# Three edits to a bidirectional recurrent stack with a ternary FFN: the fold's sums on VectorE, small statistics on GpSimd, and an earlier end of the last FC chunks

## The chip, the cores and the metric

The kernel runs on one core of a Trainium2 chip. Its time is device microseconds of one execution, and the median of a few executions is quoted. Of the kernel before there are three timed runs (1719.25, 1719.33 and 1719.43 us) and one execution under the hardware profiler. The core has a matrix engine (TensorE, PE in the profile), a vector engine (VectorE, DVE), an activation engine (ScalarE, ACT), a general engine (GpSimd, POOL) and a queue engine that issues transfers (SyncE, SP). Each engine takes its instructions in order and waits for the others by semaphores.

## The reference

The input x has 8 sequences of 512 tokens with 512 features. Two residual blocks are applied in turn. Norms without gamma and beta are plain.

```
h0   = layernorm(x)
fwd  = stack(h0);  bwd = flip(stack(flip(h0)))        # the same weights in both directions
stack: for i in 0..3:
    z  = sigmoid(h @ Wz[i].T + bz[i]);  t = tanh(h @ Wh[i].T + bh[i])
    a  = clip(1 - z);   h_new = linear_scan(a, z * t)     # along the tokens
    h  = layernorm(h_new + (h if i > 0 else 0)) * gamma + beta
x    = x + concat(fwd, bwd) @ fusion_W + fusion_b
g    = gelu(layernorm(x) @ ternary(W_fc).T);  x = x + (layernorm(g) * ln_w + ln_b) @ ternary(W_proj).T
```

Wz and Wh are one and the same matrix here, and so are bz and bh. A layer thus has one product u, and its three gate factors a, t and z all come from that u. ternary() rounds a matrix to -1, 0, 1 by a threshold from its mean absolute value.

## The kernel before

**Tiles.** 512 features make four chunks (NC_ = 4) of 128 partitions, 512 tokens make four tiles (NT = 4), and the 2048 hidden features of the FFN make 16 chunks (NF). The state of one sequence in one direction, called an item here, is kept with features on partitions (h, 128x4x512), as the scan along the tokens wants it. The layernorm needs tokens on partitions, so each layer ends with a turn there and back.

**Slots.** The recurrent stage is written out by hand as a list of slots (`slot`, L439). A slot of a layer issues one chunk of the product (`gates`, L456: four fp32 matmuls, each of which PE runs as two passes of 512 columns), the three activations of that chunk (`factors`, L475), VectorE's clamp and product (`product`, L483), the scan (L489) and the residual addition (L548). Beside that it takes shares of the norm of an item before it (`shares`, L258). Eight sequences run in four pairs. In a pair, each layer runs over four items: both directions of both sequences.

**The norm.** `norm` (L340) queues four token tiles and then four feature chunks. For each tile, PE makes four transposes into PSUM (pt, L316; two buffers). `stats` (L168) has VectorE find mean and variance (bn_stats, bn_aggr into mv, L171 and L173), add the epsilon (ve, L177) and negate the mean (nmu, L182), and GpSimd take the power -0.5 (rs, L178). `normalise` (L185) then has ScalarE multiply nmu by rs (nmr, L188) and write the normalised tile to SBUF (tok, L189). When four such tiles exist, PE turns them back (pf, L325) and ScalarE applies gamma and beta (L331). In most slots one tile is turned. In some, called two-tile slots here, two tiles are turned; PE's queue then holds transposes behind the second of them which wait for a tok. The same `stats` serves the tokens of x at the front (rx), the last layer, where only rs is wanted (rsv, since the norm's shift is folded into the fusion's weights), and the tokens of y in the FFN (rs_y, nmr_y; `y_stats` and `y_tokens`, L923 to L931).

**The fold.** The last layer's gamma, beta and mean are folded into the fusion's weights fw (two directions of four chunks of 128x512) and bias fb. `fold_sums` (L663) makes PE sum each direction's fw, weighted by gamma and by beta, over all 512 rows: four fp32 matmuls into pfold, copied to SBUF by ScalarE (L673). It is called after layer 1 of the first two items. The tile `both` (L119, filled at L729) holds the weights; the two `fpick` tiles choose a row. `fold` (L675), in layer 2, spreads the mean over the partitions with one matmul (pm, L678) and has VectorE correct the four chunks (L682). `fold_bias` (L685) does the same for the bias with two matmuls (pb, L688) and an addition (L689). The two sums sit in tok buffers meanwhile, and the counter `held` says so to the slots, which admit a new token tile only below 10.

**The rest of the recurrent stage.** `fusion` (L567) multiplies the last layer's states by fw (pu, L582), and VectorE scales by rsv and adds (L592). The first layer of the next pair (L504) is interleaved with it. Work on the FFN's weights (absolute sums, thresholds, ternary values) is taken in pieces along the recurrent stage.

**The FFN.** One step per hidden chunk: `fc` (L831) makes eight passes on PE (ph, L836), ScalarE's gelu, square and scaled copy (ghi), and VectorE's two running sums (L851) and glo (L853). Two steps later `proj` (L858) makes eight passes into the four po tiles. `token_stats` (L868) turns the running sums into a mean and a scale for each token. At the end of the list the FC chunks are doubled up in two steps (L939), so that `token_stats` of the last sequence comes two steps before the end (L943). `center` (L893) and `finish_last` (L915) are VectorE's last work on each token tile, and `store` (L900) sends the tile out on SP's queue.

Of the kernel before, what the change touches and what calls it, by code (L numbers as in the profile page):

```python
# [9 lines left out]
F32 = mybir.dt.float32  # L10
F32R = mybir.dt.float32r
AF = mybir.ActivationFunctionType
ALU = mybir.AluOpType
# [3 lines left out]
P = 128  # L17
# [7 lines left out]
def kernel(  # L25
# [84 lines left out]
    fb = const.tile([P, H], F32, name="fb")  # L110
    lnw = const.tile([P, NF], F32, name="lnw")
    lnb = const.tile([P, NF], F32, name="lnb")

# [2 lines left out]
    nc.vector.memset(warm, 0.0)  # L116
    ones = const.tile([P, P], F32, name="ones")
    nc.vector.memset(ones, 1.0)
    both = const.tile([P, NC_, 2, 64], F32, name="both")  # L119
    picks = []  # L120
    for i in range(2):
        s = const.tile([P, P], F32, name=f"fpick{i}")
        nc.vector.memset(s, 0.0)
        nc.vector.memset(s[64 * i : 64 * i + 1, :], 1.0 / H if i else 1.0)
        picks.append(s)


    xT[0] = hp.tile([P, NC_, S], F32, tag="h", name="xT_0")
# [39 lines left out]
    def stats(src, name, rs=None, shift=True):  # L168

        st = small.tile([P, 6], F32, tag="st", name=f"st_{name}")  # L170
        nc.vector.bn_stats(st, src)  # L171
        mv = small.tile([P, 2], F32, tag="mv", name=f"mv_{name}")
        nc.vector.bn_aggr(mv, st)  # L173
# [3 lines left out]
        nc.vector.tensor_scalar(ve, mv[:, 1:2], LN_EPS, None, ALU.add)  # L177
        nc.gpsimd.tensor_tensor(rs, ve, mhalf, ALU.pow)  # L178
        if not shift:
            return rs, None  # L180
        nmu = small.tile([P, 1], F32, tag="nmu", name=f"nmu_{name}")
        nc.vector.tensor_scalar(nmu, mv[:, 0:1], -1.0, None, ALU.mult)  # L182
        return rs, nmu

    def normalise(dst, src, rs_nmu, name):  # L185
        rs, nmu = rs_nmu
        nmr = small.tile([P, 1], F32, tag="nmr", name=f"nmr_{name}")
        nc.scalar.activation(nmr, nmu, AF.Copy, scale=rs)  # L188
        nc.scalar.activation(dst, src, AF.Identity, bias=nmr, scale=rs)  # L189

    def ternary(dst, w, hi_lo):
# [37 lines left out]
    with rec:  # L229
# [428 lines left out]
                extra.append([None, lambda hi=hi, lo=lo, v=v: nc.vector.tensor_tensor(lo, v, hi.bitcast(F32), ALU.subtract)])  # L658


        folded = {}

        def fold_sums(d):  # L663

            ps = ps_u.tile([P, H], F32, tag="u", name=f"pfold_{d}")
            for c in range(NC_):
                nc.tensor.matmul(
                    ps, lhsT=both[:, c, :, :].rearrange("p i r -> p (i r)"), rhs=fw[:, d * NC_ + c, :],
                    start=(c == 0), stop=(c == NC_ - 1),
                )  # L670
            folded[d] = tokp.tile([P, H], F32, tag="tok", name=f"fold_{d}")
            held[0] += 1
            nc.scalar.copy(folded[d], ps)  # L673

        def fold(d):  # L675

            pm = ps_u.tile([P, H], F32, tag="u", name=f"pm_{d}")
            nc.tensor.matmul(pm, lhsT=picks[1], rhs=folded[d], start=True, stop=True)  # L678
            for c in range(NC_):
                def chunk(c=c):  # L680
                    w = fw[:, d * NC_ + c, :]
                    nc.vector.scalar_tensor_tensor(w, w, gam[:, c : c + 1], pm, ALU.mult, ALU.subtract)  # L682
                stages.append((now[0] + c, "resid", chunk))

        def fold_bias():  # L685
            pb = ps_u.tile([P, H], F32, tag="u", name="pb")
            for d in range(2):
                nc.tensor.matmul(pb, lhsT=picks[0], rhs=folded[d], start=(d == 0), stop=(d == 1))  # L688
            nc.vector.tensor_tensor(fb, pb, fb, ALU.add)  # L689
            held[0] -= 2  # L690


        def load_pair(use, b):
# [34 lines left out]
        for i, v in enumerate((bet, gam)):  # L728
            nc.vector.tensor_copy(both[:, :, i, :], v.unsqueeze(2).broadcast_to([P, NC_, 64]))  # L729
        for b in range(0, B, 2):  # L730
            last_pair = b + 2 == B
            if b == 0:
                for name, part in (("fc", fc_part), ("pw", proj_part)):
                    for i in range(NW):
                        absolute(part, i, name)
                    tots = []
                    extra.append([None, lambda n=name, tots=tots: tots.append(total(n))])
                    extra.append([None, lambda n=name, tots=tots: threshold(n, tots[0])])
                for name, part in (("fc", fc_part), ("pw", proj_part)):
                    for i in range(NW):  # L740
                        quantised(part, i, name)
            for l in range(1, L):
                if last_pair:
                    load_fc(l - 1)
                    if l == 1:
                        combined()
                        load_pw(0)
                for s in ((b, 0), (b, 1), (b + 1, 0), (b + 1, 1)):
                    if l == L - 1 and not last_pair and s[1] == 0:
                        norm_x(s[0] + 2, now[0])  # L750
                    if l == L - 1 and s[1] == 0:
                        load_pair("f", s[0])
                    if l == L - 2 and not last_pair and s[1] == 1:
# [7 lines left out]
                    if b == 0 and l == 1 and s[0] == 0:  # L761
                        fold_sums(s[1])
                    if b == 0 and l == 2:
                        if s[0] == 0:
                            fold(s[1])
                        elif s[1] == 0:
                            fold_bias()
            if last_pair:
                load_fc(L - 1)


            firsts = [] if last_pair else first_layer(b + 2) + first_layer(b + 3)
            for i in range(2):
                for t, tile_ in enumerate(fusion(b + i)):
                    slot(tile_, 2, True)
                    for _ in range(2 if i == 0 and t % 2 == 0 else 1):
                        if firsts:
                            slot(firsts.pop(0))
                if last_pair and i == 0:
                    load_pw(1)  # L780
                    load_pw(2)
# [132 lines left out]

    def finish_last(b, t):  # L915
        row = xs["y", b, t]
        nc.vector.scalar_tensor_tensor(row, po[b][t], stat[b][0][:, t : t + 1], row, ALU.mult, ALU.add)
        store(b, t)

    rests = []  # L920
    found, ytok = {}, {}
# [97 lines left out]
```

## Time and profile before

| | us |
|---|---|
| median of three runs | 1719.33 |
| the profiled execution's own time | 1719.44 |
| its span in the profile | 1717.4 |
| time of that execution outside the span | 2.0 |
| PE busy | 1705.8 |
| VectorE busy | 1449.8 |
| ScalarE busy | 1072.3 |
| GpSimd busy | 214.5 |

| stretch, us | PE busy | VectorE busy | ScalarE busy | GpSimd busy |
|---|---|---|---|---|
| 0 to 62 (loads, first layer) | 57.62 | 50.11 | 40.92 | 10.63 |
| 62 to 111 (pair 0, layer 1) | 47.56 | 42.97 | 39.55 | 8.43 |
| 111 to 230 (pair 0, layers 2 and 3) | 118.86 | 109.84 | 102.27 | 19.41 |
| 230 to 1222 (pairs 1 to 3 and fusions) | 990.8 | 876.8 | 597.3 | 148.4 |
| 1222 to 1717 (FFN) | 491.00 | 370.02 | 292.32 | 27.63 |

In a line of the groups, the form is: source line, engine, operation, output and input by the program's names, sizes, count, then the busy time in us and the mean in ns of one instruction, then the idle time of the engine just before such instructions and what ended it. In a timeline, each line has start and duration in us. A line with a count above one stands for several instructions that followed each other without a gap.

### The profile page before, as it was taken

What the parts mean: (1) busy time and instruction counts of PE and PEld (TensorE: products, weight loads), DVE (VectorE), ACT (ScalarE), POOL (GpSimd) and SP (SyncE); (2) the same over time, 40 slices, a digit from 0 to 9 for tenths busy, and PEclk for the clock granted to TensorE, in tenths of its full rate; (3) what the DMA queues carried; (4) which work ended last, traced back from release to release, by engine and by line L of the source; (5) the groups of instructions that cost most, each with busy time, mean ns of one, the idle gap of its engine ahead of it and who ended that gap; (6) DMA issues with size and microseconds to landing.
All of it is one profiled execution on the core that took longest, in us unless ns stands there. A gap on an engine that the chain in (4) does not pass through costs nothing.

```text
span 1717.4 us, 19766 instructions
## 1 busy us (share of the span) xinstructions
PE 1705.8 (99%) x6442; PEld 1042.8 (61%) x6442; DVE 1449.8 (84%) x2859; ACT 1072.3 (62%) x1851; POOL 214.5 (12%) x334
## 2 busy tenths in 40 slices
PE   9999999999999999999999999999999999999998
PEld 4455554555555455555545555554688888888887
DVE  7989989889998998999899899996568768768876
ACT  5898883468886246888624688861266566566654
POOL 2111111111111111111111111110000000000000
PEclk9999999999999999999999999999999999999999
DMA  7002221160000115000012200202201101100100
GB/s 270 19 25 81 99 86 43 56 202 1 1 13 19 56 59 199 1 1 19 13 55 68 105 15 35 74 1 98 74 1 49 50 1 50 50 19 32 50 19 31
DMA packets 46455, 91.75 MB, mean 53 GB/s; under 512 B 5264, under 2 KB 5264, under 8 KB 45328
## 3 DMA queue, kind: packets, MB, share of 16 engines
q1 hardware_dynamic: 45632, 89.18, 15.3%
q10 hardware_dynamic: 720, 1.31, 0.2%
q8 instruction: 51, 0.84, 0.2%
q14 instruction: 52, 0.43, 0.1%
HBM read 65.30 MB, written 25.17 MB: 53 GB/s over the span
## 4 chain that ended last, share of the span: by engine, by line
PE 85%; DVE 9%; issue 4%; ACT 1%; DMA 1%; POOL 0%; DVEq 0%; POOLq 0%; ACTq 0%; SPq 0%
PE u L461 33%; PE pu L582 12%; PE ph L836 12%; PE po L863 12%; PE pt L316 6%; PE u L504 5%; PE pf L325 4%; DVE z L489 2%; DVE st L171 1%; DVE z L485 1%; PE py L214 1%; DVE zf L489 1%; DVE z L548 1%; DVE a L484 1%; DMA xT<-in_xt_dram 0%
## 5 line engine op out<-in xcount | busy, mean ns | idle before, releaser
L461 PE MATMUL u<-h,gw 128*128 128x512 f32 x768 | 345.5, 592 | 0.0
L461 PE MATMUL u<-xT,gw 128*128 128x512 f32 x768 | 345.4, 593 | 0.0
L489 DVE TENSOR_TENSOR_SCAN z<-a,z 128x512 f32<-128x512 f32 x224 | 274.1, 1224 | 7.6
L840 ACT ACTIVATE g<-ph 128x512 f32<-128x512 f32 x128 | 76.4, 597 | 240.6 <-PE ph L836 240.6
L461 PEld LDWEIGHTS u<-h,gw 128*128 128x128 f32 x768 | 138.7, 190 | 139.2 <-issue 138.9
L461 PEld LDWEIGHTS u<-xT,gw 128*128 128x128 f32 x768 | 138.7, 190 | 139.2 <-issue 138.2
L478 ACT ACTIVATE a<-u,ngb 128x512 f32<-128x512 f32 x192 | 131.6, 685 | 142.2 <-PE u L461 141.6
L171 DVE BATCH_NORM_STATS2 st<-pt 128x6 f32<-128x512 f32 x256 | 177.1, 692 | 40.5 <-PE pt L316 40.1
L178 POOL TENSOR_TENSOR rs<-ve,mhalf 128x1 f32<-128x1 f32 x192 | 123.2, 642 | 702.8 <-DVE nmu L182 669.9
L863 PE MATMUL po<-pwq,ghi 128*128 128x512 f32 x512 | 203.5, 398 | 0.0
L836 PE MATMUL ph<-yhi,fcq 128*128 128x512 f32 x512 | 199.7, 390 | 0.0
L863 PE MATMUL po<-pwq,glo 128*128 128x512 f32 x512 | 199.6, 390 | 0.0
L836 PE MATMUL ph<-ylo,fcq 128*128 128x512 f32 x512 | 199.4, 389 | 0.0
L485 DVE TENSOR_TENSOR z<-z,t 128x512 f32<-128x512 f32 x224 | 153.4, 685 | 9.1 <-ACT z L480 9.1
L189 ACT ACTIVATE tok<-pt,nmr,rs 128x512 f32<-128x512 f32 x192 | 149.2, 777 | 6.4
L851 DVE TENSOR_TENSOR acc<-acc,g 128x512 f32<-128x512 f32 x112 | 77.3, 690 | 87.9 <-ACT g L840 87.0
L480 ACT ACTIVATE z<-u,gb 128x512 f32<-128x512 f32 x192 | 132.2, 689 | 0.0
L479 ACT ACTIVATE t<-u,gb 128x512 f32<-128x512 f32 x192 | 130.7, 681 | 0.0
L316 PEld LDWEIGHTS pt<-ident,z 128*128 128x128 f32 x640 | 78.6, 141 | 79.7 <-issue 47.7
L504 PE MATMUL u<-xT,gw 128*128 128x512 f32 x256 | 114.8, 593 | 0.8 <-DVE gw L711 0.8
L582 PE MATMUL pu<-fw,xT 128*128 128x512 f32 x256 | 115.2, 593 | 0.0
L582 PE MATMUL pu<-fw,h 128*128 128x512 f32 x256 | 115.1, 592 | 0.0
(147 smaller groups left out, 2558.5 us busy)
## 6 DMA issues: line engine op xcount, KB each, us to landing
xn<-in_x_dram SPq DMA_DIRECT2D x32, 256.0 KB, 4.4
xf<-in_x_dram SPq DMA_DIRECT2D x32, 256.0 KB, 5.5
x<-xf SPq DMA_DIRECT2D x32, 256.0 KB, 2.0
xy<-x SPq DMA_DIRECT2D x32, 256.0 KB, 4.4
out_dram<-xy SPq DMA_DIRECT2D x32, 256.0 KB, 2.0
xT<-in_xt_dram SPq DMA_DIRECT2D x7, 1024.0 KB, 7.5
fca<-in_fc_wT_dram SPq DMA_DIRECT2D x16, 256.0 KB, 3.0
pwa<-in_proj_wT_dram SPq DMA_DIRECT2D x16, 256.0 KB, 2.6
```

The source lines that it names most:

```text
L171: nc.vector.bn_stats(st, src)
L189: nc.scalar.activation(dst, src, AF.Identity, bias=nmr, scale=rs)
L316: nc.tensor.transpose(pt[:, ts(c, P)], zs[c][:, ts(t, P)], ident)
L461: nc.tensor.matmul(u, lhsT=gw[l][:, c, ts(o, P)], rhs=h[:, c, :], start=(c == 0), stop=(c == NC_ - 1),)
L478: nc.scalar.activation(a, u, AF.Sigmoid, bias=ngb[:, l, o : o + 1], scale=-1.0)
L480: nc.scalar.activation(z, u, AF.Sigmoid, bias=gb[:, l, o : o + 1])
L485: nc.vector.tensor_tensor(z, z, t, ALU.mult)
L489: nc.vector.tensor_tensor_scan(dst[:, d], a[:, d], z[:, d], 0.0, ALU.mult, ALU.add)
L504: nc.tensor.matmul(u, lhsT=gw[0][:, c, ts(o, P)], rhs=xT[b][:, c, :], start=(c == 0), stop=(c == NC_ - 1),)
L582: nc.tensor.matmul(pu, lhsT=hs[d][:, c, ts(t, P)], rhs=fw[:, d * NC_ + c, :], start=(c == 0), stop=(c == NC_ - 1),)
L836: nc.tensor.matmul(ph, lhsT=w, rhs=ys[b][c][i], start=(c == 0 and i == 0), stop=(c == NC_ - 1 and i == 1),)
L863: nc.tensor.matmul(po[b][t], lhsT=part[:, ts(t, P)], rhs=pwq[k // NP_][:, k % NP_, :], start=(k == 0 and i == 0), stop=(k == NF - 1 and i ...
```

## The change

It has three parts, in one diff.

**The fold.** `fold_sums`, `fold` and `fold_bias` are replaced by one function `fold()`, which is called once, after layer 1 of the first item. It queues 16 VectorE instructions of 128x512, one for every second slot: for each direction, four that sum gamma times chunk into `sum_g`, and four that sum beta times chunk into `sum_b`. These are sums over chunks alone; the sum over partitions is left to the matmul that spreads it. After each direction's sums `centred` issues the one pm matmul and queues the four corrections of fw; last comes `bias` with one pb matmul. The tile `both`, its two copies and the fpick tiles go; `mean_of` and `sum_b` come.

**The statistics.** In `stats`, ve is made by GpSimd, nmu is gone, and nmr is made by GpSimd as mean times rs times -1. `normalise` is left with one ScalarE instruction.

**The end.** The doubling of FC chunks starts two steps earlier and covers three steps; `token_stats` of the last sequence comes one step earlier. The last token tile is finished in two halves, the second half stored from ScalarE's queue. The pool of ghi and glo has six buffers instead of five.

```diff
-    both = const.tile([P, NC_, 2, 64], F32, name="both")
-    picks = []
...
+    mean_of = fusp.tile([P, P], F32, name="mean_of")
+    nc.vector.memset(mean_of, 1.0 / H)
+    sum_b = fusp.tile([P, H], F32, name="sum_b")
...
-        nc.vector.tensor_scalar(ve, mv[:, 1:2], LN_EPS, None, ALU.add)
+        nc.gpsimd.tensor_scalar(ve, mv[:, 1:2], LN_EPS, None, ALU.add)
         nc.gpsimd.tensor_tensor(rs, ve, mhalf, ALU.pow)
         if not shift:
             return rs, None
-        nmu = small.tile([P, 1], F32, tag="nmu", name=f"nmu_{name}")
-        nc.vector.tensor_scalar(nmu, mv[:, 0:1], -1.0, None, ALU.mult)
-        return rs, nmu
...
-        nc.scalar.activation(nmr, nmu, AF.Copy, scale=rs)
+        nc.gpsimd.tensor_scalar(nmr, mv[:, 0:1], rs, -1.0, ALU.mult, ALU.mult)
+        return rs, nmr
...
-        folded = {}
-        def fold_sums(d):
...
+        def fold():
+            sum_g = qp.tile([P, H], F32, tag="q", name="sum_g")
+            at = [now[0]]
+            def later(f):
+                stages.append((at[0], "resid", f))
+                at[0] += 2
+            def summed(dst, w, v, first):
+                if first:
+                    later(lambda: nc.vector.tensor_scalar(dst, w, v, None, ALU.mult))
+                else:
+                    later(lambda: nc.vector.scalar_tensor_tensor(dst, w, v, dst, ALU.mult, ALU.add))
+            def centred(d):
+                pm = ps_u.tile([P, H], F32, tag="u", name=f"pm_{d}")
+                nc.tensor.matmul(pm, lhsT=mean_of, rhs=sum_g, start=True, stop=True)
+                for c in range(NC_):
...
+                    stages.append((now[0] + c, "resid", chunk))
+            def bias():
+                pb = ps_u.tile([P, H], F32, tag="u", name="pb")
+                nc.tensor.matmul(pb, lhsT=ones, rhs=sum_b, start=True, stop=True)
+                nc.vector.tensor_tensor(fb, pb, fb, ALU.add)
             for d in range(2):
+                for dst, v in ((sum_g, gam), (sum_b, bet)):
+                    for c in range(NC_):
+                        summed(dst, fw[:, d * NC_ + c, :], v[:, c : c + 1], c == 0 and (dst is sum_g or d == 0))
+                later(lambda d=d: centred(d))
+                at[0] += NC_ - 2
+            later(bias)
...
-    partp = ctx.enter_context(tc.tile_pool(name="parts", bufs=5, reuse_waits="tile"))
+    partp = ctx.enter_context(tc.tile_pool(name="parts", bufs=6, reuse_waits="tile"))
...
-        nc.vector.scalar_tensor_tensor(row, po[b][t], stat[b][0][:, t : t + 1], row, ALU.mult, ALU.add)
-        store(b, t)
+        for h in range(2 if t == NT - 1 else 1):
+            cols = slice(h * H // 2, (h + 1) * H // 2) if t == NT - 1 else slice(0, H)
+            nc.vector.scalar_tensor_tensor(
+                row[:, cols], po[b][t][:, cols], stat[b][0][:, t : t + 1], row[:, cols], ALU.mult, ALU.add
+            )
+            (nc.scalar if h else nc.sync).dma_start(out=out[b, ts(t, P), cols], in_=row[:, cols])
...
-        for _ in range(2 if ends - 4 <= j < ends - 2 else 1):
+        for _ in range(2 if ends - 6 <= j < ends - 3 else 1):
...
-        if j == ends - 2:
+        if j == ends - 3:
             late.append(token_stats(b))
```

More of the change, by code (lines that the diff above doesn't have):

```diff
@@ L109 @@
     bet = const.tile([P, NC_], F32, name="bet")
-    fb = const.tile([P, H], F32, name="fb")
+    fb = fusp.tile([P, H], F32, name="fb")
     lnw = const.tile([P, NF], F32, name="lnw")
@@ L118 @@
     nc.vector.memset(ones, 1.0)
-    both = const.tile([P, NC_, 2, 64], F32, name="both")
-    picks = []
[L121 to L125, printed above, removed]
+    mean_of = fusp.tile([P, P], F32, name="mean_of")
+    nc.vector.memset(mean_of, 1.0 / H)
+    sum_b = fusp.tile([P, H], F32, name="sum_b")
     xT[0] = hp.tile([P, NC_, S], F32, tag="h", name="xT_0")
@@ L180, in stats, with normalise @@
             return rs, None
-        nmu = small.tile([P, 1], F32, tag="nmu", name=f"nmu_{name}")
-        nc.vector.tensor_scalar(nmu, mv[:, 0:1], -1.0, None, ALU.mult)
-        return rs, nmu
-    def normalise(dst, src, rs_nmu, name):
-        rs, nmu = rs_nmu
         nmr = small.tile([P, 1], F32, tag="nmr", name=f"nmr_{name}")
-        nc.scalar.activation(nmr, nmu, AF.Copy, scale=rs)
+        nc.gpsimd.tensor_scalar(nmr, mv[:, 0:1], rs, -1.0, ALU.mult, ALU.mult)
+        return rs, nmr
+    def normalise(dst, src, rs_nmr, name):
+        rs, nmr = rs_nmr
         nc.scalar.activation(dst, src, AF.Identity, bias=nmr, scale=rs)
@@ L658, in combined @@
                 extra.append([None, lambda hi=hi, lo=lo, v=v: nc.vector.tensor_tensor(lo, v, hi.bitcast(F32), ALU.subtract)])
-        folded = {}
-        def fold_sums(d):
[L665 to L686, printed above, removed]
-            for d in range(2):
-                nc.tensor.matmul(pb, lhsT=picks[0], rhs=folded[d], start=(d == 0), stop=(d == 1))
-            nc.vector.tensor_tensor(fb, pb, fb, ALU.add)
-            held[0] -= 2
+        def fold():
[13 more added lines that the diff above has]
+                for c in range(NC_):
+                    def chunk(c=c):
+                        w = fw[:, d * NC_ + c, :]
+                        nc.vector.scalar_tensor_tensor(w, w, gam[:, c : c + 1], pm, ALU.mult, ALU.subtract)
+                    stages.append((now[0] + c, "resid", chunk))
[3 more added lines that the diff above has]
+                nc.vector.tensor_tensor(fb, pb, fb, ALU.add)
+            for d in range(2):
+                for dst, v in ((sum_g, gam), (sum_b, bet)):
[4 more added lines that the diff above has]
+            later(bias)
@@ L727 @@
             slot(work, 4 if i == NC_ + 1 else 2, i > NC_ + 1)
-        for i, v in enumerate((bet, gam)):
-            nc.vector.tensor_copy(both[:, :, i, :], v.unsqueeze(2).broadcast_to([P, NC_, 64]))
         for b in range(0, B, 2):
@@ L760 @@
                     layer(s, l)
[L761 to L767, printed above, removed]
+                    if (b, l, s) == (0, 1, (0, 0)):
+                        fold()
             if last_pair:
```

## The prediction

> **What bounds the kernel now.** I read the busy shares and the chain of waits first, then PE's own waits, then the groups that the diff touches, and last the timeline where PE waits.
>
> ```profile
> PE 1705.8 (99%) x6442; PEld 1042.8 (61%) x6442; DVE 1449.8 (84%) x2859; ACT 1072.3 (62%) x1851; POOL 214.5 (12%) x334
> ...
> PE 85%; DVE 9%; issue 4%; ACT 1%; DMA 1%; POOL 0%; DVEq 0%; POOLq 0%; ACTq 0%; SPq 0%
> ```
>
> PE is busy for 1705.8 of 1717.4 us. So a pass removed from PE is worth its time, unless PE then waits, and any new wait of PE is a loss. PE's waits, by what ended them (total us, times, longest):
>
> ```profile
> PE pt L316 <- ACT tok L189: 2.5, 7, 0.6
> PE pt L316 <- DVE z L489: 1.3, 1, 1.3
> ...
> PE pf L325 <- ACT tok L189: 0.4, 1, 0.4
> ```
>
> The commonest wait is that of transposes for tok, the end of the chain of statistics that the diff rebuilds. The groups that it touches:
>
> ```profile
> L178 POOL TENSOR_TENSOR rs<-ve,mhalf 128x1 f32<-128x1 f32 x192 | 123.2, 642 | 702.8 <-DVE nmu L182 669.9 <-DVE a L484 15.9 <-ACT z L480 12.1
> L188 ACT ACTIVATE nmr<-nmu,rs 128x1 f32<-128x1 f32 x192 | 56.7, 295 | 74.6 <-POOL rs L178 64.9 <-DVE st L171 5.7 <-DVE xf L592 1.6
> L177 DVE TENSOR_SCALAR ve<-mv 128x1 f32<-128x1 f32 x256 | 39.3, 153 | 26.3 <-DVE mv L173 0.5
> L182 DVE TENSOR_SCALAR nmu<-mv 128x1 f32<-128x1 f32 x192 | 27.6, 144 | 0.5 <-issue 0.5
> L667 PE MATMUL pfold<-fw,both 128*128 128x512 f32 x16 | 7.2, 592 | 0.0
> L682 DVE SCALAR_TENSOR_TENSOR fw<-fw,gam,pm 128x512 f32<-128x512 f32 x8 | 5.9, 740 | 0.0
> L688 PE MATMUL pb<-fold,fpick 128*128 128x512 f32 x4 | 1.9, 593 | 0.0
> ```
>
> A two-tile slot, in the timeline from 371.5 us on. The second tile's mean and variance are there at 372.43 (bn_aggr from 372.25, 0.18 long):
>
> ```profile
> 371.69 0.55 POOL L178 TENSOR_TENSOR rs<-ve,mhalf 128x1 f32<-128x1 f32 x1 [3.40 <-DVE nmu L182]
> ...
> 372.67 0.42 DVE L484 TENSOR_SCALAR a<-a 128x512 f32<-128x512 f32 x1
> 372.84 0.66 POOL L178 TENSOR_TENSOR rs<-ve,mhalf 128x1 f32<-128x1 f32 x1 [0.60 <-DVE nmu L182]
> ...
> 373.00 0.69 DVE L485 TENSOR_TENSOR z<-z,t 128x512 f32<-128x512 f32 x1
> ...
> 373.72 1.23 DVE L489 TENSOR_TENSOR_SCAN z<-a,z 128x512 f32<-128x512 f32 x1
> 373.85 0.78 ACT L189 ACTIVATE tok<-pt,nmr,rs 128x512 f32<-128x512 f32 x1
> ...
> 374.69 0.66 PE L316 MATMUL pt<-ident,z 128*128 128x128 f32 x4 [0.23 <-ACT tok L189]
> ```
>
> The second power takes 0.66 us, not 0.55. It began inside the clamp `a`, and it ended at 373.50, which is 0.41 after the clamp's end at 373.09. Begun inside a scan, a power takes longer still (timeline at 38 us), though GpSimd has the same work:
>
> ```profile
> 38.24 1.45 POOL L178 TENSOR_TENSOR rs<-ve,mhalf 128x1 f32<-128x1 f32 x1 [0.59 <-DVE nmu L182]
> ```
>
> So GpSimd is stopped by the VectorE instruction in flight. That is the one thing in the profile that speaks against this change.
>
> **What the Trainium skill says.** "SBUF — State Buffer", section "Who interferes with whom": a VectorE instruction with two SBUF inputs, or one in a two-port mode, holds a port which GpSimd's reads need, and the other "fully blocks". The trace agrees: 0.55 us beside bn_stats, which reads PSUM, 0.66 and 1.45 us beside the clamp and the scan, and the clamp keeps its 0.42. "GPSIMD Engine Reference", section 2.1 "Instruction dispatch": the next GpSimd instruction does not wait for the one before, so a dependent one needs a semaphore wait; the built order of the changed kernel has these waits between ve, power and nmr. "Perfetto Trace Analysis", section "GPSIMD Engine Instruction": GpSimd's spans are unreliable, so I use them against VectorE's ends only.
>
> **The fold.** PE loses two pfold groups of eight passes and two of pb's four: 18 passes. A pass counts start to start, not by its 592 ns: pfold runs from 88.58 us and the next product starts at 92.02, so 3.44 us for eight, 0.43 each, and 18 x 0.43 = 7.74 us. ScalarE loses two copies of 0.58, VectorE two of 0.28. VectorE gains 16 instructions of 128x512. No such sum is in the trace; the nearest row, L682, takes 740 ns, and bounds from the clamp (0.42) to L194's like form (0.75) would give 6.7 to 12 us. I take 16 x 0.74 = 11.8 us. One falls in every second slot, so 0.37 us a slot. A slot lasts 4.31 us on PE (eight passes, 3.44, and eight transposes of 0.109), and VectorE is busy 110 of 119 us in 111 to 230: about 0.33 us a slot free. That isn't enough alone, but the second part gives back more, so I cost the sums at nothing. Without that cover they would cost 16 x 0.74 - 40 slots x 0.33, about nothing to 2 us. The corrections and pm move later, still ahead of the fusion; they keep their price. With the sums out of the tok pool, one transpose tile comes a slot sooner: nothing.
>
> **The statistics.** VectorE loses ve (0.15) on every tile and nmu (0.14) on most. Start to start, bn_aggr to ve takes 0.29 us (372.25 to 372.54) and nmu to the next 0.06, so 0.33 to 0.42 us leave a tile's chain, about 0.35 a slot with one tile: as much as the fold's sums take. ScalarE loses 224 nmr of 0.295, 66 us, which lie beside PE's work and are no gain as such. GpSimd gets 317 ve and 224 nmr. A 128x1 tensor_scalar on GpSimd isn't in the trace: from below, its memset of the same size takes 98 ns; from above, the power 0.55. I take 0.1 to 0.2, nearer to the memset; the skill's only GpSimd timings are for long rows, and don't help.
>
> What matters is when tok can start. Behind nmr, ScalarE's in-order queue holds tok and then the next slot's a, t and z, for which VectorE waits; behind a late ve, GpSimd's queue holds the next tile's three instructions. In a one-tile slot the turn back waits for a tok made a slot earlier, about 1.0 us of room: most of a delay is hidden, and I leave 0.3 us for the few slots without room. In a two-tile slot the second tok is on PE's path. With GpSimd never stopped: bn_aggr's end 372.43, 0.15 for the semaphore, ve 0.1, power 0.55, nmr 0.1 and two handovers of 0.03: tok at 373.4 instead of 373.85. PE had waited 0.23, so the slot gains up to 0.3. With GpSimd stopped at each step: ve in the clamp, the power in the product, nmr in the scan, so tok 0.41 after the scan's end. VectorE is 0.35 earlier by then: (373.72 + 1.23 - 0.35) + 0.41 = 375.0, which is 1.2 us later than before. So a two-tile slot costs -0.3 to +1.2, and I take +0.3: ve may get through in the gap ahead of the clamp, and then the power ends where it did. I count 12 such slots with PE near its wait: nine in the first pair (at about 41, 47, 73, 78, 84, 89, 103, 108 and 125 us), and one in each later first layer (at about 374, 672 and 971). That is 12 x 0.3 = 3.6 us.
>
> **The end.** Last, in the timeline:
>
> ```profile
> 1711.57 2.72 DVE L917 SCALAR_TENSOR_TENSOR xy<-po,rsg,xy 128x512 f32<-128x512 f32 x4
> ...
> 1712.34 2.31 SPq L901 DMA_DIRECT2D out_dram<-xy  x4
> ```
>
> The last pass starts at 1712.61, ends at 1713.0, and VectorE finishes at 1714.29. It is late because `center` ran to 1711.65. A step of eight passes is 8 x 0.227 = 1.82 us, so statistics one step sooner let each finish start at its tile's end, and the last half ends about 0.9 us after PE instead of 1.3. The half-size store is shorter too. ScalarE's queue is empty there, so its store waits behind nothing. Bounds 0.4 to 1.0; I take 0.7. The passes that move are the same in number, and the sixth buffer keeps the third early chunk from waiting.
>
> **Sum,** against the profiled execution's 1719.44: -7.74 + 3.6 + 0.3 - 0.7 = -4.5, so 1714.9 us; against the median of 1719.33, 1714.8.
>
> **Rivals.** (A) GpSimd is hardly stopped: two-tile slots at -0.1 on average, nothing in the others: -7.74 - 1.2 - 0.7 = -9.6, so 1709.8. For it: the short instructions may slip between two of VectorE's. Against it: 0.66 and 1.45. (B) GpSimd is stopped three times in each two-tile slot: 12 x 1.2 = 14.4, with 1.1 in the one-tile slots ahead of norms without room: -7.74 + 15.5 - 0.7 = +7.1, so 1726.5. It is slower from 0.7 us a slot on, and by more than 0.2% from 1.0 on. For it: VectorE's clamp, product, scan and addition follow without a gap. Against it: PE's waits there were below 0.6, and a slot late by 1.2 leaves the next with fewer things to wait for. (C) The fold's gain isn't realised: at 63.9 us, VectorE runs without a gap from 65 to 71, so PE that comes 3.44 sooner only waits for z: -4.5 + 3.4, so 1718.3, no change that can be told.
>
> **How the numbers follow.** A measurement of this kernel can tell about 0.2%, 3.4 us, from no change: below 1715.9 is faster, above 1722.8 slower. Chances: my forecast 0.35 (its own range 1711 to 1719), A 0.25, B 0.25, C 0.15. Of the forecast's 0.35, 0.24 lie below 1715.9; A gives 0.25; C 0.02: faster 0.51. C's rest and the forecast's rest give 0.22 for no change with 0.02 of B; slower is the rest, 0.27 with C's tail. A with the end at 1.0 and its slots at -0.2 gives 1708.3, and B with every slot stopped gives 1726.5, beyond which other stages would have to be late too. The range from 1708.5 to 1726.5 leaves out about half of B and a little of A, 0.15 to 0.2.
>
> **What would show it.** PE busy must fall by about 7.7 (the fold). PE's waits for tok should total 4 to 7 us instead of 2.9; near 15 is B, below 2 is A. In a two-tile slot, the time from bn_aggr's end to the second tok was 1.42 us: 1.0 is A, near 1.7 mine, 2.6 B. The waits of PE for z in the first 111 us tell C. The time from PE's last pass to the end of the span, 4.4 us, should become 3.7. I am wrong if GpSimd's tensor_scalar takes over 0.4, or if VectorE becomes late in 77 to 230 us.

## The result, and the profile after

The changed kernel takes 1743.83 us (median of 4 runs, 1743.39 to 1745.07) against 1719.37 us of the kernel before in the same sessions (1719.25 to 1719.43). The ratio is 1.0143, with a 95% interval of 1.0126 to 1.0161. It is 24.5 us slower. The forecast was 1714.8, with a range that ended at 1726.5.

The page of the changed kernel, busy shares and chain:

```profile
PE 1708.1 (98%) x6424; PEld 1042.3 (60%) x6424; DVE 1403.3 (81%) x2330; ACT 1007.7 (58%) x1625; POOL 474.5 (27%) x875
...
PE 56%; issue 22%; POOL 14%; DVE 4%; ACT 3%; DMA 1%; POOLq 0%; DVEq 0%
```

VectorE and ScalarE have less to do, as the diff intends (46.5 and 64.6 us less). GpSimd has 260 us more. GpSimd had 0% of the chain that ended last before; now it has 14%. PE has 18 passes fewer, and yet is busy 2.3 us longer: some passes ran at half the clock (below). PE's waits, total, times and longest:

```profile
PE pt L310 <- ACT tok L183: 15.7, 14, 4.0
PE pf L319 <- ACT tok L183: 11.0, 11, 2.3
```

Waits for tok were 2.9 us before; they are 26.7 us now, beyond even the 15 us that the prediction had named for rival B. The groups of the statistics, and the wait of tok's engine:

```profile
L183 ACT ACTIVATE tok<-pt,nmr,rs 128x512 f32<-128x512 f32 x192 | 149.6, 780 | 210.5 <-POOL nmr L178 210.4
...
L174 POOL TENSOR_TENSOR rs<-ve,mhalf 128x1 f32<-128x1 f32 x192 | 147.5, 768 | 16.1 <-POOL ve L173 0.2
...
L178 POOL TENSOR_SCALAR nmr<-mv,rs 128x1 f32<-128x1 f32 x192 | 105.2, 548 | 19.9
...
L173 POOL TENSOR_SCALAR ve<-mv 128x1 f32<-128x1 f32 x256 | 77.8, 304 | 741.8 <-DVE mv L169 715.0 <-ACT z L474 11.8 <-ACT t L473 7.2
```

The power's mean grew from 642 to 768 ns though it is the same instruction. nmr takes 548 ns where ScalarE took 295. Why is seen in the two-tile slot of pair 1, the same slot as in the prediction, in the timeline of the changed kernel:

```profile
386.66 0.82 POOL L174 TENSOR_TENSOR rs<-ve,mhalf 128x1 f32<-128x1 f32 x1
386.95 0.18 DVE L169 BATCH_NORM_AGGREGATE mv<-st 128x2 f32<-128x6 f32 x1
387.05 0.39 DVE L478 TENSOR_SCALAR a<-a 128x512 f32<-128x512 f32 x1
387.36 0.68 DVE L479 TENSOR_TENSOR z<-z,t 128x512 f32<-128x512 f32 x1
387.58 0.59 POOL L178 TENSOR_SCALAR nmr<-mv,rs 128x1 f32<-128x1 f32 x1
388.08 1.22 DVE L483 TENSOR_TENSOR_SCAN z<-a,z 128x512 f32<-128x512 f32 x1
...
388.26 1.06 POOL L173 TENSOR_SCALAR ve<-mv 128x1 f32<-128x1 f32 x1
...
389.34 0.69 DVE L542 TENSOR_TENSOR z<-z,xT 128x512 f32<-128x512 f32 x1
389.40 1.05 POOL L174 TENSOR_TENSOR rs<-ve,mhalf 128x1 f32<-128x1 f32 x1
389.95 0.69 DVE L167 BATCH_NORM_STATS2 st<-pt 128x6 f32<-128x512 f32 x1
390.56 0.27 POOL L178 TENSOR_SCALAR nmr<-mv,rs 128x1 f32<-128x1 f32 x1
...
390.86 0.78 ACT L183 ACTIVATE tok<-pt,nmr,rs 128x512 f32<-128x512 f32 x1 [1.87 <-POOL nmr L178]
...
391.69 0.66 PE L310 MATMUL pt<-ident,z 128*128 128x128 f32 x4 [1.99 <-ACT tok L183]
```

Read it as a staircase. The first tile's power begins in time, but VectorE's clamp, which now starts 0.10 us after the start of the second tile's bn_aggr instead of 0.42, starts while it runs, and the power ends with the clamp (387.48, the clamp at 387.44). The first tile's nmr ends 0.13 after the product (388.17 and 388.04). Only then may the second tile's ve begin, inside the scan, and it ends with the scan (389.32 and 389.30). The second power begins inside the residual addition and ends 0.42 after it (390.45 and 390.03). The second nmr begins beside the end of bn_stats, which reads PSUM, and takes its own 0.27. The second tok begins 3.73 us after its bn_aggr ended (387.13); before it was 1.42. PE waits 2.0 us; before it was 0.23. The 3.73 us lie between the ends and starts of VectorE's and ScalarE's instructions, so they don't hang on GpSimd's spans.

The end, in the timelines of VectorE and ScalarE:

```profile
1739.55 0.88 DVE L915 SCALAR_TENSOR_TENSOR xy<-po,rsg,xy 128x256 f32<-128x256 f32 x2 [0.15 <-PE po L858]
```

```profile
1740.46 0.35 ACTq L918 DMA_DIRECT2D out_dram<-xy  x1
```

VectorE now waits for PE's last tile; before, it was late itself, behind `center`. From PE's last end, 1739.52, to the end of the span, 1743.3, are 3.8 us instead of 4.4.

### The profile page after: what moved, and what is told of

Its sections match the earlier page's. It is cut to its first block, busy times and chain, and to the rows that moved or that the text cites. A ratio compares the mean times of both kernels' runs of the same rounds, so it can differ in the third digit from the quotient of the medians.

```text
span 1743.3 us, 19460 instructions
## 1 busy us (share of the span) xinstructions
PE 1708.1 (98%) x6424; PEld 1042.3 (60%) x6424; DVE 1403.3 (81%) x2330; ACT 1007.7 (58%) x1625; POOL 474.5 (27%) x875
## 4 chain that ended last, share of the span: by engine, by line
PE 56%; issue 22%; POOL 14%; DVE 4%; ACT 3%; DMA 1%; POOLq 0%; DVEq 0%
PE u L455 17%; PE po L858 13%; PE ph L831 13%; POOL rs L174 6%; PE pu L576 5%; POOL nmr L178 4%; POOL ve L173 3%; PE pt L310 2%; PE u L498 2%; PE pf L319 2%; DVE z L483 1%; PE py L208 1%; ACT tok L183 1%; DVE zf L483 1%; DVE st L167 1%
## 5 line engine op out<-in xcount | busy, mean ns | idle before, releaser
L455 PE MATMUL u<-xT,gw 128*128 128x512 f32 x768 | 348.8, 597 | 0.0
L173 POOL TENSOR_SCALAR ve<-mv 128x1 f32<-128x1 f32 x256 | 77.8, 304 | 741.8 <-DVE mv L169 715.0
L479 DVE TENSOR_TENSOR z<-z,t 128x512 f32<-128x512 f32 x224 | 154.4, 689 | 43.4 <-ACT z L474 37.7
L174 POOL TENSOR_TENSOR rs<-ve,mhalf 128x1 f32<-128x1 f32 x192 | 147.5, 768 | 16.1 <-POOL ve L173 0.2
L319 PE MATMUL pf<-ident,tok 128*128 128x128 f32 x768 | 113.9, 274 | 11.2 <-ACT tok L183 11.0
L498 PE MATMUL u<-xT,gw 128*128 128x512 f32 x256 | 116.4, 600 | 0.8 <-DVE gw L713 0.8
```

What stands on the lines that cost most here:

```text
L319: nc.tensor.transpose(pf[:, ts(t, P)], toks[t][:, ts(c, P)], ident)
L455: nc.tensor.matmul(u, lhsT=gw[l][:, c, ts(o, P)], rhs=h[:, c, :], start=(c == 0), stop=(c == NC_ - 1),)
L479: nc.vector.tensor_tensor(z, z, t, ALU.mult)
L498: nc.tensor.matmul(u, lhsT=gw[0][:, c, ts(o, P)], rhs=xT[b][:, c, :], start=(c == 0), stop=(c == NC_ - 1),)
```

## The experiments

Kernels named here keep their own line numbers, which differ by a few. Where a run leaves out work, the expectation says which.

**One part at a time (e1 to e4).** Four kernels, each with one part of the diff, or two. e1 takes the statistics' part alone, e2 the fold's, e3 the end's, and e4 the whole diff without the statistics' part:

```diff
 e4: the changed kernel with
-        nc.gpsimd.tensor_scalar(ve, mv[:, 1:2], LN_EPS, None, ALU.add)
+        nc.vector.tensor_scalar(ve, mv[:, 1:2], LN_EPS, None, ALU.add)
...
-        nc.gpsimd.tensor_scalar(nmr, mv[:, 0:1], rs, -1.0, ALU.mult, ALU.mult)
+        nc.vector.tensor_scalar(nmu, mv[:, 0:1], -1.0, None, ALU.mult)
 and nmr made by ScalarE in normalise, as before
```

> The kernel before with the statistics' small operations on GpSimd alone (ve and nmr there, nmu gone), fold and end as before. Theory T (the chain of three GpSimd instructions, each held up by VectorE's port, makes tok late, PE waits, and after long waits PE's clock falls): the whole loss is here, +25 to +36 us against before, so 1744 to 1755 us, with a second tok about 2 us later in the two-tile slot of a later pair. Rival F (the fold's 16 sums are too much for VectorE in the first pair, and the late tok there follows from that): under +8 us, at most 1727, and PE's waits in the first 230 us near those of before.

> The kernel before with the fold's sums on VectorE alone; statistics and end as before. Theory T: PE loses 7.74 us of passes and VectorE's 16 sums find room, so -5 to -8 us: 1711 to 1714. Rival F: VectorE becomes late between 77 and 230 us, PE waits for z or tok there, and the kernel is slower than before by 5 us or more. Rival C of the prediction (gain hidden at the first removed group, since VectorE is the bound there): -3 to -5 us.

> The kernel before with the early end alone: doubled FC chunks two steps sooner, statistics one step sooner, the last tile in two halves, six buffers of parts (the fold's constants and bias tile sit in the fusion's pool for room). Both theories: 0.4 to 1.0 us faster, 1718.4 to 1719.0; from PE's last pass to the end of the span 3.8 us instead of 4.4. If the extra early chunks made PE wait, it would be equal or slower.

> The changed kernel with the statistics put back to VectorE and ScalarE; fold and end as changed. Theory T: -6 to -9 us against before, 1710.5 to 1713.5, with PE's waits for tok near the 2.9 us of before. Rival F: slower than before, since the statistics' relief of VectorE is gone and the sums stay: above 1725.

| run | median us | before, same session | difference | ratio, 95% interval |
|---|---|---|---|---|
| e1, statistics alone | 1740.49 | 1719.20 | +21.3 | 1.0125 [1.0111, 1.0139] |
| e2, fold alone | 1722.94 | 1719.20 | +3.7 | 1.0023 [1.0014, 1.0031] |
| e3, end alone | 1718.80 | 1719.20 | -0.4 | 0.9998 [0.9990, 1.0006] |
| e4, fold and end | 1722.49 | 1719.20 | +3.3 | 1.0019 [1.0012, 1.0027] |

The three parts add up: 21.3 + 3.7 - 0.4 = 24.6, and the change measures 24.5. So in sum the parts neither help nor hurt each other by more than the noise, and I explain each by itself. The statistics are the greater part of the loss, though not all of it, as theory T had it (25 us or more). The fold, the part with the sure gain on PE, loses too: e2 and e4 lie between the bands of T, F and C, and none of the three is right as it stood. The gain at the end is of the size foreseen, but its interval includes no change.

**Where the fold's gain went (e5 to e7).** The first thing to look at is PE at the place of the first removed group, in e2's timeline:

```profile
72.05 0.69 DVE L167 BATCH_NORM_STATS2 st<-pt 128x6 f32<-128x512 f32 x1
...
75.11 0.66 PE L312 MATMUL pt<-ident,zf 128*128 128x128 f32 x4 [3.29 <-ACT tok L185]
...
77.26 3.95 PE L457 MATMUL u<-h,gw 128*128 128x512 f32 x6
```

The kernel before at the same place:

```profile
72.05 0.69 DVE L171 BATCH_NORM_STATS2 st<-pt 128x6 f32<-128x512 f32 x1
...
75.10 0.66 PE L316 MATMUL pt<-ident,zf 128*128 128x128 f32 x4
```

bn_stats starts at 72.05 in both. VectorE does not notice that PE came 3.44 us sooner: it works without a gap from 65 us on, and PE waits 3.3 us for what it would have met ready. And after that wait, six passes take 3.95 us, where six took 2.74 in the kernel before (at 371.28 us). The page "TensorE: Matmul & The Clock Gate" of the Trainium skill says in its section "What's actually happening" that PE's clock is gated by how busy it was; the trace agrees, with passes 0.85 us apart instead of 0.43 after waits that come to about 2 us and more within a few us. In the changed kernel 15 passes after 30 us have that spacing, about 6.4 us in all; in the kernel before none.

Three runs on e2 take the rest apart:

```diff
 e5: e2 with 13 of the 16 sums left out
-                    later(lambda: nc.vector.scalar_tensor_tensor(dst, w, v, dst, ALU.mult, ALU.add))
+                    at[0] += 2
 e6: e2, after fold() is called
+                        idle2 = ps_u.tile([P, H], F32, tag="u", name="idle2")
+                        for c in range(NC_):
+                            nc.tensor.matmul(idle2, lhsT=mean_of, rhs=fw[:, c, :], start=(c == 0), stop=(c == NC_ - 1))
 e7: e2, ahead of the threshold's piece
+                    extra.append([None, lambda: None])
```

> The fold alone (as e2), but 13 of the 16 VectorE sums are left out: only the first of each row is made, so the fused weights lack the rest. If e2's loss is the sums' load on VectorE between 77 and 230 us, this run is faster than e2 by most of their 9.6 us, with the waits at 135 to 228 us gone: about 1715 to 1717. If the loss is only the empty gain at 71 us with the clock's fall after it, the sums cost nothing and the time stays within 1 us of e2's 1722.9.

> The fold alone (as e2), and in the place of the first removed group four matmuls whose result nobody reads (eight passes, 3.4 us of PE). If PE only waited in that place, and the wait made its clock fall for the next slot, the added work costs nothing and even gains 1 to 2 us: 1721 to 1722. If the clock's fall costs nothing, equal to e2. If the removed group had been worth its time, +3.4 us: 1726.4.

> The fold alone (as e2), but with one empty piece between VectorE's total of the absolute sums and the threshold's matmul, so that PE meets that matmul at least a slot later than the total. If the 2 us wait at 207 us and the slow passes after it are a loss by themselves, -3 to -4 us against e2: 1719 to 1720. If VectorE's lateness in this stretch is the bound in any case, the wait turns up at the next transposes, and the time stays within 1 us of e2.

e5 measured 1717.42 us, 5.5 below e2 and 2.0 below before (0.9990 [0.9982, 0.9999]). So 13 of the 16 sums that I had costed at nothing cost 5.5 us, and even without them only 2.0 of the 7.74 us arrive. e6 measured 1722.98, equal to e2 (1722.94): eight passes put back in the first place are free. So the first group was worth nothing, and the clock's fall at 77 us cost nothing there either, since without it PE only waits a little later, for tok at 80 to 88 us. My expectation of a gain from e6 missed. e7 measured 1724.45 us, 1.5 above e2, with intervals that overlap. The wait at the threshold went, and one of 3.1 us came at the next turn back (pf, up to 228 us). So that wait was no loss by itself: VectorE was late there, and PE had to wait for it at one instruction or the next.

**Which of the two moved operations costs (e8 and e9).**

```diff
 e8: the changed kernel with
-        nc.gpsimd.tensor_scalar(ve, mv[:, 1:2], LN_EPS, None, ALU.add)
+        nc.vector.tensor_scalar(ve, mv[:, 1:2], LN_EPS, None, ALU.add)
 e9: e4 with
-        nc.vector.tensor_scalar(ve, mv[:, 1:2], LN_EPS, None, ALU.add)
+        nc.gpsimd.tensor_scalar(ve, mv[:, 1:2], LN_EPS, None, ALU.add)
```

> The changed kernel with ve put back to VectorE; power and nmr on GpSimd (nmu gone, ScalarE's nmr gone). Theory T (each instruction of the chain on GpSimd is held up once more by VectorE's port): two steps instead of three, so about half of the statistics' 21.3 us is gone: 1731 to 1735. If ve alone was the trouble (it stands behind the first tile's nmr in GpSimd's queue): 1724 to 1727. If GpSimd's nmr was (it takes 0.55 us in place of ScalarE's 0.30, and stands between the power and tok): above 1738.

> The changed kernel with nmu on VectorE and nmr on ScalarE as before; ve and power on GpSimd. To be set beside e4 (no step moved, 1722.5), e8 (nmr moved) and the changed kernel (both moved, 1743.8). Theory Q (each GpSimd step of the chain ends only after the VectorE instruction in flight ends, so what counts is whether the last step gets in ahead of the scan): the power then ends after the product instead of after the clamp, 0.7 us later, still ahead of the scan's end: +3 to +8 us on e4, 1725 to 1731. Theory O (the second tile's ve stands behind the first tile's nmr in GpSimd's queue, and only that hurts): no nmr is in the queue here, so within 2 us of e4. Theory V (ve is slow on GpSimd by itself): near the changed kernel, above 1738.

| moved to GpSimd, on e4 | median us | against e4's 1722.49 | second tok after its bn_aggr, us | PE's wait for it, us |
|---|---|---|---|---|
| nothing (e4) | 1722.49 | | 1.43 | 0.23 |
| nmr (e8) | 1719.63 | -2.9 | 1.33 | 0.11 |
| ve (e9) | 1725.63 | +3.1 | 1.91 | 0.56 |
| both (the changed kernel) | 1743.83 | +21.3 | 3.73 | 1.99 |

The last two columns are read in the two-tile slot of pair 1. e8 fell out of all three bands that I had set, on the good side; its runs spread over 3.2 us (1717.66 to 1720.88), as much as its gain. e9 lies in theory Q's band; theory V falls, and O is off by 1.1 us. Alone, the two moves cancel; together they cost 21, and the second tok comes 2.3 us later where the sum of both would be 0.4. That speaks against any price per instruction, and for a threshold. e8's timeline of the same two-tile slot, from the second tile's bn_aggr on, shows where it lies:

```profile
374.80 0.18 DVE L169 BATCH_NORM_AGGREGATE mv<-st 128x2 f32<-128x6 f32 x1
...
375.09 0.42 DVE L478 TENSOR_SCALAR a<-a 128x512 f32<-128x512 f32 x1
...
375.32 0.59 POOL L174 TENSOR_TENSOR rs<-ve,mhalf 128x1 f32<-128x1 f32 x1 [0.16 <-DVE ve L173]
375.42 0.68 DVE L479 TENSOR_TENSOR z<-z,t 128x512 f32<-128x512 f32 x1
376.01 0.27 POOL L178 TENSOR_SCALAR nmr<-mv,rs 128x1 f32<-128x1 f32 x1
376.14 1.23 DVE L483 TENSOR_TENSOR_SCAN z<-a,z 128x512 f32<-128x512 f32 x1
376.31 0.78 ACT L183 ACTIVATE tok<-pt,nmr,rs 128x512 f32<-128x512 f32 x1 [0.34 <-POOL nmr L178]
```

The power ends 0.40 after the clamp (375.91 and 375.51). nmr begins inside the product and ends 0.18 after it (376.28 and 376.10), and tok starts 0.17 us after the scan has begun. nmr's 0.27 us is no longer than what ScalarE took. So two steps on GpSimd take two of VectorE's ends. A third step behind them would have to wait out the scan, 1.22 us, as the second tile's ve does in the changed kernel.

**Is it the order on GpSimd's queue? (e10)**

```diff
 e10: the changed kernel with nmr's instruction moved from stats to normalise
+    def normalise(dst, src, rs_mv, name):
+        rs, mv = rs_mv
+        nmr = small.tile([P, 1], F32, tag="nmr", name=f"nmr_{name}")
+        nc.gpsimd.tensor_scalar(nmr, mv[:, 0:1], rs, -1.0, ALU.mult, ALU.mult)
```

> The changed kernel, but GpSimd's nmr is issued with tok instead of with the power, so that in a two-tile slot GpSimd's order is ve, power, ve, power, nmr, nmr. Theory O: the second tile's ve is free of the first's nmr, and at least 8 us of the 21 come back: below 1736. Theory Q: the second tile's chain still ends behind the scan, and the first tile's nmr now stands behind the second's power, so nothing is gained: 1741 to 1748.

It measured 1747.17 us (1.0162 [1.0148, 1.0176]), 3.3 above the changed kernel. Theory O falls; Q's band holds. The order isn't without effect, though: in the two-tile slot of pair 1 the second ve now runs beside the clamp, the second tok comes 3.0 us after its bn_aggr instead of 3.73, and PE waits 1.5 us instead of 2.0. But the first tile's nmr now stands behind the second's power, its tok starts 1.2 us later, counted from the second bn_aggr, and PE waits more elsewhere (0.98 us at 335, 638 and 941 us).

**Is it the length of the VectorE instruction? (e13 and e14)**

```diff
 e13: the changed kernel; e14: e4; both with
-            nc.vector.tensor_tensor_scan(dst[:, d], a[:, d], z[:, d], 0.0, ALU.mult, ALU.add)
+            for d in (slice(None, S // 2 - 1, -1), slice(S // 2 - 1, None, -1)) if backward else (slice(0, S // 2), slice(S // 2, S)):
+                nc.vector.tensor_tensor_scan(dst[:, d], a[:, d], z[:, d], 0.0, ALU.mult, ALU.add)
```

> The changed kernel with every scan made as two instructions of 256 columns, each starting from zero (so the recurrence is cut in the middle; the work per column is the same). Theory Q (a GpSimd step ends only after the VectorE instruction in flight; the scan is the longest): the last step gets in after half a scan, so the statistics' cost, measured as this run less e14, falls from 21.3 to 8 to 15 us. Theory N (number and own time of GpSimd's instructions): the difference to e14 stays at 19 to 23 us.

> The kernel of e4 (fold and end changed, statistics as before) with the same cut scans: what the cutting itself costs. VectorE gets 256 more instructions of some 0.06 us each, 0.06 us a slot: 1722 to 1727 against e4's 1722.5 under both theories.

e13 measured 1732.05 us and e14 1728.18. With scans of 0.68 us in place of 1.22, the same instructions on GpSimd cost 3.9 us instead of 21.3. And the changed kernel itself became 11.8 us faster, although cutting its scans gives VectorE more to do and made e4 5.7 us slower. e13's two-tile slot:

```profile
379.27 1.27 DVE L483 TENSOR_TENSOR_SCAN z<-a,z 128x256 f32<-128x256 f32 x2
...
379.45 0.53 POOL L173 TENSOR_SCALAR ve<-mv 128x1 f32<-128x1 f32 x1
380.06 0.84 POOL L174 TENSOR_TENSOR rs<-ve,mhalf 128x1 f32<-128x1 f32 x1
...
381.01 0.39 POOL L178 TENSOR_SCALAR nmr<-mv,rs 128x1 f32<-128x1 f32 x1
...
382.27 0.66 PE L310 MATMUL pt<-ident,z 128*128 128x128 f32 x4 [1.38 <-ACT tok L183]
```

The second ve takes 0.53 us where it took 1.06, and it ends at 379.98, when the first half of the scan does (379.27 and 0.69). PE then waits 1.4 us in that slot, not 2.0. The fall is larger than the 8 to 15 us that I expected to remain. PE's idle time by stretch, from 30 to 240 us (pair 0) and from 240 to 1220 us (pairs 1 to 3), is the stretch less PE's busy time there, each of one execution (e14's was 1.6 us faster than its median):

| kernel | PE idle, 30 to 240 us | PE idle, 240 to 1220 us |
|---|---|---|
| before | 3.9 | 1.2 |
| e4, none moved | 9.7 | 1.7 |
| e8, nmr moved | 9.0 | 1.6 |
| e9, ve moved | 12.1 | 2.9 |
| the changed kernel, both | 18.2 | 10.4 |
| e14, none moved, scans cut | 11.8 | 5.2 |
| e13, both moved, scans cut | 13.2 | 8.4 |

The cost of moving both falls in each: from 8.5 to 1.4 us in pair 0, and from 8.7 to 3.2 us in the later pairs. But cutting the scans alone adds 2.1 and 3.5 us of idle time (e14 is 5.7 us above e4, more than I allowed), and where PE waits for VectorE in any case, a late chain costs less. So some of the fall may be overlap, and how much was not separated. The 11.8 us by which the changed kernel gained are free of this doubt, though part of them comes by way of PE's clock: passes 0.85 us apart are 15 in the changed kernel and 5 in e13. Theory N, for which the number of GpSimd's instructions or their own time is the cost, expected neither.

**Versions from what was found (e11, e12 and e15).** e11 is the kernel before with nmr on GpSimd and the early end. e12 adds half of the fold: the first direction's sums stay on PE, where they are free, and the second's 8 sums go to VectorE, one in every third slot. e15 starts the second direction's sums one item sooner, one in every second slot, and places the corrections of the weights behind them at the same pace:

```diff
 e12, on e11
+                    if (b, l, s) == (0, 1, (0, 0)):
+                        fold_sums(0)
+                    if (b, l, s) == (0, 1, (0, 1)):
+                        fold_second()      # 8 sums of direction 1, then centred(1) and bias()
 e15, on e12
+                means[d] = qp.tile([P, H], F32, tag="q", name=f"mean_{d}")
+                nc.scalar.copy(means[d], pm)
...
+                    later(lambda d=d, c=c: chunk(d, c))
```

> The kernel before with two things alone: nmr on GpSimd (ve on VectorE, nmu gone), and the early end. No fold change. Theory Q: the power ends at the clamp's end and nmr at the product's end, ahead of the scan, and the waits for the second tok in the later pairs' two-tile slots (0.39 us, three times) and in pair 0 shrink, as they did from e4 to e8 (-2.9 us): -2.5 to -4 us against before, 1715.3 to 1717. If e8's gain came only from VectorE's relief under the fold's sums: within 1 us of e3, 1718 to 1719.

> As e11, and half of the fold: the first direction's sums stay on TensorE, where PE had to wait for VectorE in any case; the second direction's 8 sums go to VectorE, one for every third slot. PE saves one group of eight passes (3.44 us). If the second group was worth its time (PE is the bound after 88 us) and 8 spread sums cost nothing: 3 us below e11, 1712 to 1714. If VectorE has no room even for these: at e11 or slower.

> As e12 (nmr on GpSimd, early end, first direction's sums on TensorE, second's on VectorE), with the corrections of the weights placed one in every second slot behind the sums, from a copy of pm in SBUF made by ScalarE, so that no slot holds more than one added VectorE instruction. If e12's two waits (1.2 us at 169 and 2.5 us at 222 us) came from slots with two or three such additions, 3 us below e11: 1714 to 1715. If VectorE has no room in the first pair for any added work, no gain on e11's 1717.3.

e11 measured 1717.26 us (0.9989 [0.9981, 0.9997]), 2.1 below before: faster than both kernels. It lies between the two bands, 0.3 us from theory Q's. Some 1.6 us of it are nmr's, if e3's 0.4 is the end's; so what e8 gained beyond that may be relief of VectorE under the fold's sums. e12 measured 1717.92 (0.9993 [0.9985, 1.0001]) and e15 1717.49 (0.9988 [0.9981, 0.9994]): 3.44 us less for PE to do, and nothing that can be told gained on e11. e12's PE waits 1.0 us for tok at 170 us, behind a slot with two added VectorE instructions, and 2.4 us at 225 us, where there is one (a correction at 220.5 us). e15 has neither wait, but others, of 1.2 us for tok at 104 us and 0.7 us at the threshold. So VectorE in pair 0 had no room even for half of the sums in either placing.

## Why the prediction was wrong

Set beside the terms of the sum, with one part at a time: the fold was taken at -7.74 and measured +3.7 us (e2), the statistics at +3.9 (3.6 and 0.3) and measured +21.3 (e1), the end at -0.7 and measured -0.4 (e3).

**The step that failed: the price of a slot on GpSimd.** The prediction gave a two-tile slot "-0.3 to +1.2" and took +0.3. It had read the right mechanism from the trace, that GpSimd is stopped by the VectorE instruction in flight, and rival B was built on it. But in the three later two-tile slots PE's wait grew from 0.23 to 2.0 us, by 1.8, beyond even the upper bound. Two things were left out of the count. The first tile's nmr stands ahead of the second tile's ve in GpSimd's queue, so the second chain begins not in the clamp but in the scan: four steps in a row from the product on, not three from the clamp on. And VectorE, rid of ve and nmu, starts its clamp sooner, so that even the first tile's power is caught. I had entered that (0.35 us; it came to 0.32) as a gain for the chain. e10 shows that another order on the queue is no cure by itself. e8 and e9 show that with either step alone tok still starts before the scan's end, and e13 that a shorter scan costs less: what decides is the count of steps against VectorE's longest instruction. One of the prediction's own signs said as much: GpSimd's nmr takes 0.55 us on average, over the 0.4 from which I was to be wrong.

**"About 1.0 us of room" in a one-tile slot.** This was taken to hide most of the delay there, and 0.3 us was left for it. PE's wait at the turn back (pf) is 11.0 us in the changed kernel and 2.1 in e4, so this term was mis-sized too, by about 8.6 us; the waits at the transposes (pt) grew by 11.1 us, from 4.6 to 15.7. Together that is 20.0 us, nearly all of the statistics' 21.3. 6.4 us of the pf waits stand in pair 0 from 126 to 220 us, and 2.3 in one place in pair 3. The room is real, as no such waits stand in most slots of the later pairs. That it is too short in pair 0 because VectorE itself runs late there is likely, but was not tested by itself.

**"So I cost the sums at nothing."** 13 of the 16 cost 5.5 us (e2 less e5). The prediction named the cover, the relief by the statistics' part. But e1, e2 and e3 simply add up to the whole, so the relief covered nothing that can be measured. Part of what VectorE got back it spent waiting: its waits for ScalarE's z ahead of the product rose from 9.1 to 37.7 us. ScalarE makes z behind tok, in order; that this is the reason was not tested by itself.

**"18 x 0.43 = 7.74 us."** The passes went, but the first group's 3.44 us were empty. Rival C said so, at 0.15, from the line that VectorE runs without a gap there; it should have been the main case, since VectorE's 92% in pair 0 was on the table. C had PE wait for z; it waited for tok, whose chain begins on VectorE too. With 13 of the 16 sums gone, the fold is worth 2.0 us (e5), where 4.3 would be left without the first group; what holds back the rest was not separated.

**What held.** The end: 0.7 taken, 0.4 measured, and from PE's last pass to the end of the span 0.3 us less in e3's trace and 0.6 in the changed kernel's. The direction of the port's effect held too: the power's 0.41 after the clamp is seen again in e8 (0.40).

**A step that was not there: PE's clock.** Every wait of PE was priced at its own length. After long waits 15 passes ran at half clock, 6.4 us in sum. e6 shows one such place where that cost nothing. e4 has 7 such passes, 3.0 us, so the statistics add 8. How much of the change's 24.5 us it makes elsewhere was not separated.

## What to carry to other kernels

Before a small step is moved to GpSimd, lay its chain beside VectorE's instructions and count: each dependent GpSimd step may need one end of a VectorE instruction on SBUF, so ask which is the longest instruction that the last step could fall behind. One step more or less around that point was worth 18 to 24 us here (both moves less one of them), while each move by itself was worth 3, one for the better and one for the worse. And a pass taken from the busiest engine is worth its time only where that engine is the bound: compare, slot by slot, when the next engine starts, before the removed work is counted as a gain.

## What the runs showed of the hardware

GpSimd's 128x1 tensor_scalar, by its span in the profile, takes 0.22 us (one scalar) to 0.27 us (two) beside a bn_stats, which reads PSUM, or an idle VectorE, and up to 1.25 us when it meets a scan (nmr at 37.09 us in the changed kernel). In the slots read here it ends 0.02 to 0.14 us after the VectorE instruction that lengthened it; the power ends 0.36 to 0.42 us after. A power already under way was still lengthened by a clamp that began 0.39 us later (0.82 us in place of 0.55), while the clamp kept its 0.39. The Trainium skill's "SBUF — State Buffer", section "Who interferes with whom", lets whoever issues first hold the port for the whole instruction; here the measurement decides, and VectorE came through although it was second. It wasn't slowed elsewhere either: in the changed kernel the 165 scans that began at least 0.1 us into a GpSimd instruction lasted 1.22 us like the other 91, and 42 such clamps 0.40 us like the other 182. PE's clock halved after waits of about 2 us in some places and not in others: of the three like slots at 389, 690 and 991 us, only the last was followed by slow passes.
